# The rests of a split matrix product as float16 instead of float32r, with a re-drawn instruction list

## The chip, the cores and the metric

The kernel runs on one core of a Trainium2 chip. The metric is the device time of one execution in microseconds (us). TensorE is PE in the profile, its loads of the stationary operand are PEld, VectorE is DVE, ScalarE is ACT, GpSimd is POOL, and SP issues the DMAs.

## What is computed

The inputs are x (2 x 1024 x 2048), a context of 2 x 2048 x 2048, a 0/1 matrix `kernel` (2048 x 2048, one entry in ten is 1) and a few scalars. The reference in short:

```python
def fake_quant(x, s, z):
    return (clip(round(x / s + z), 0, 255) - z) * s

x = x + tanh(g_xattn) * (fake_quant(layernorm(x), ...) @ fake_quant(ctx, ...))
y = layernorm(x)                                   # the new x
y = concat([y[..., :1638], -4.0 * y[..., 1638:]])  # 0.8 of the 2048 columns stay
x = x + tanh(g_ffn) * scale * (y @ kernel)
```

So there are two products of 2048 rows by 2048 by 2048. The operands of the first are small integers and go through TensorE as float16 without loss. The left factor of the second is a real float32 matrix, here called A.

## The kernel before

**Tiling.** The 2048 rows are 16 tiles of 128 rows; two tiles make a pair p (0 to 7), two pairs make a product q (0 to 3). All large buffers in SBUF are pages of 4 KB per partition, 44 in all (`page`, `PAGES`). PSUM has three accumulators of 128 x 1024 (`acc`) and two of 128 x 512 (`tr`).

**First product.** Batch 0 is computed directly (`mm1`, line 544) and so is half of batch 1; the other half goes by Strassen's scheme (`mm1s`, line 646), in seven products of halves M1 to M7. All are float16 matmuls of 128 x 128 by 128 x 512. Column sums of the context come from matmuls with ones (lines 556 and 574).

**Second product**, the one that the change touches. For each q the kernel works in Strassen's scheme again:
- `reload2`/`scale2` (line 685) normalise a tile; `factor` (lines 447 to 453) has made the factor r, by a reciprocal and one correction step e.
- `turn2` (line 692) transposes it on TensorE, `take2` (lines 704, 706) moves it from PSUM to a page A, and `combine` (lines 722 to 728) makes the sums of halves.
- `part_hi` (line 738, ACT) rounds A to float32r, and `part_lo` (line 742, DVE or POOL) takes the rest, A - hi, into a page of its own, also as float32r. Each left factor (m, p) has one hi and one lo page.
- `load_w` fetches the right factor as bytes, four k-blocks per page, and `widen` (line 782, ACT) turns each block of 128 x 1024 into float32r (`wf`). The entries are small integers.
- `mm2` (line 809) is the step of TensorE: for one pair and one k-block it issues four matmuls, hi with the left and the right 512 columns, then lo with the same. There are 4 x 7 x 2 x 8 = 448 such steps.
- `add2` (line 825, DVE) adds the accumulator times f2 to a page `back`, and `store2` writes it out.

**The order of the work.** Nothing is scheduled by a compiler. The kernel first describes all operations with their costs, reads, writes and buffers (`op`). `Plan.run` then simulates the engines in units of about a 16-bit matmul's time: each engine takes the ready operation that is due earliest. An operation becomes ready when those it depends on have ended, plus a lag that depends on the releasing engine (`"PE": 6.0`). `Plan.order` repeats this with changed due times (80 tries), keeps the best end, and the instructions are issued in that order, so each engine's queue is fixed when the program is built. A page is opened by one operation and is free when all its users have ended.

Of the kernel before, what the change touches and what calls it, by code (L numbers as in the profile page):

```python
# [22 lines left out]
HB = 1024  # L23
EPS = 1e-5
UNIT = 2.0**-24
CENTER = 128.0
PAGES = 44

# [6 lines left out]
class Plan:  # L35
# [77 lines left out]
    def order(self, lag, start, runs, seed=1):  # L113


        self.dues()
        chance = random.Random(seed)
        free, count = dict(self.free), dict(self.count)
        dues = [o.due for o in self.ops]
        best = None  # L120
        for i in range(runs):
            self.free, self.count = dict(free), dict(count)
            try:
                end = self.run(lag, start)
            except RuntimeError:
                end = None
            if end is not None and (best is None or end <= best[0]):
                best = end, self.began, [o.engine for _, _, o in self.began]
                dues = [o.due for o in self.ops]
                held = self.held_up()  # L130
            for o, due in zip(self.ops, dues):
                o.due = due
            for ops in held:
                if chance.random() < 0.5:
                    step = chance.choice((3.0, 6.0, 12.0, 24.0))
                    for o in ops:
                        o.due -= step
            if i % 3:
                place = chance.uniform(0.0, self.place)
                for o in self.ops:  # L140
                    if o.place is None and abs(o.due - place) < 120.0 and chance.random() < 0.1:
                        o.due += chance.uniform(-25.0, 25.0)
        _, self.began, engines = best
        for (_, _, o), e in zip(self.began, engines):
            o.engine = e
        return [o for _, _, o in self.began]
# [133 lines left out]
def gated_xattn_ffn_kernel(  # L280
# [26 lines left out]

    nc = tc.nc  # L310
    B, S, D = x.shape
    K = kv.shape[1]
# [65 lines left out]
    nc.vector.tensor_scalar(kc12, c1, -CENTER, None, ALU.add)  # L378
    nc.vector.tensor_scalar(kc12, kc12, f1c2, float(K), ALU.mult, ALU.mult)
    f2 = const.tile([P, 1], F32, name="f2")  # L380
    nc.vector.tensor_scalar(f2, gate[:, 1:2], sc[:, 6:7], None, ALU.mult)

    ident = const.tile([P, P], F32, name="ident")
    make_identity(nc, ident)
# [56 lines left out]
    def factor(v, t: int):  # L441


        va, sd = root.pop((v, t))
        mean = mv[v, t][:, 0:1]
        r0 = small.tile([P, 1], F32, tag="r0", name=f"r0_{v}{t}")
        nc.vector.reciprocal(r0, sd)

        e = small.tile([P, 1], F32, tag="e", name=f"e_{v}{t}")
        nc.vector.tensor_scalar(e, r0, r0, va, ALU.mult, ALU.mult)  # L450
        nc.vector.tensor_scalar(e, e, -0.5, 1.5, ALU.mult, ALU.add)
        r = small.tile([P, 1], F32, tag="r", name=f"r_{v}{t}", bufs=T)
        nc.vector.tensor_scalar(r, r0, e, None, ALU.mult)
        fac[v, t] = (r, mean)
        if v == "a":
            w = small.tile([P, 1], F32, tag="w", name=f"w_{v}{t}")
            nc.vector.tensor_scalar(w, va, r, zs1, ALU.mult, ALU.mult)
            nc.vector.tensor_scalar(w, w, mean, None, ALU.subtract)
            nc.vector.tensor_scalar(r, r, rs1, None, ALU.mult)
            wr = small.tile([P, 1], F32, tag="wr", name=f"wr_{v}{t}")  # L460
            nc.vector.tensor_scalar(wr, w, r, None, ALU.mult)
            fac[v, t] = (r, w, wr)
# [275 lines left out]
        nc.scalar.copy(hi[m, p], A[left(m, p)])  # L738

    def part_lo(m: str, p: int, engine=None):  # L740
        lo[m, p] = page([KH, P], F32R, f"lo_{m}_{p}")
        engines[engine].tensor_sub(lo[m, p], A[left(m, p)], hi[m, p].bitcast(F32))  # L742


    RIGHT = {"M1": ("B11", 0), "M2": ("B21", 0), "M3": ("B22", 0), "M4": ("T4", 2),
# [54 lines left out]
    def mm2(q: int, m: str, p: int, k: int, js=(0, 1)):  # L800
        if m in OPENS and k == 0 and apart(p, m):
            acc2[SUM[m], p] = [ps_tr.tile([P, NB], F32, tag="tr", name=f"acc2_{m}_{p}_{j}") for j in range(2)]
        elif m in OPENS and k == 0:
            acc = ps_acc.tile([P, 2, NB], F32, tag="acc", name=f"acc2_{m}_{p}")
            acc2[SUM[m], p] = [acc[:, j, :] for j in range(2)]
            acc2[SUM[m], p, 0] = flat(acc)
        for part in (hi, lo):
            for j in js:
                nc.tensor.matmul(  # L809
                    acc2[SUM[m], p][j],  # L810
                    part[m, p][:, k, :],
                    wf[q, m, k][:, ts(j, NB)],
                    start=(m in OPENS and k == 0 and part is hi),
                    stop=(k == KH - 1 and part is lo),
                    skip_group_check=True,
                )

# [209 lines left out]
    def ops_parts(m: str, p: int):  # L1027
        a = ("A",) + left(m, p)
        op({"ACT": ACT(HB)}, part_hi, m, p, reads=both(a), writes=[(("hi", m, p), 0)],
           opens=[("page", ("hi", m, p))], lead=60)  # L1030
        op({"DVE": DV2(HB), "POOL": GPS(HB)}, part_lo, m, p, reads=[*both(a), (("hi", m, p), 0)],
           writes=[(("lo", m, p), 0)], opens=[("page", ("lo", m, p))], lead=60, port=True)

    def ops_combine(p: int):
        t, u = 2 * p, 2 * p + 1
# [17 lines left out]
    def ops_product2(q: int, between):  # L1053
        pairs = (2 * q, 2 * q + 1)
        for n, m in enumerate(ORDER):
            for j in range(2):
                name = RIGHT[m][0]
                op({"SP": DMA}, load_w, q, m, j, reads=[(("wt", name, j), 0)] if name[0] == "T" else [],
                   writes=[(("wr", q, m, j), 0)], opens=[("page", ("wr", q, m, j))], lead=45)
            for k in range(KH):  # L1060
                w = ("wf", q, m, k)
                op({"ACT": ACT(HB)}, widen, q, m, k, reads=[(("wr", q, m, k // 4), 0)], writes=[(w, 0)],
                   opens=[("page", w)], lead=14)
            if n == 0:
                for p in pairs:
                    ops_combine(p)
            elif n + 1 < len(ORDER):
                for p in pairs:
                    ops_parts(ORDER[n + 1], p)
            if m in FIRST:  # L1070
                for p in pairs:
                    v = ("back", p) + TAKES[m]
                    op({"SP": DMA}, load_back, p, *TAKES[m], reads=[(("kept", 2 * p + TAKES[m][0], TAKES[m][1]), 0)],
                       writes=both(v), opens=[("page", v)], due=plan.place + 50, lead=50)
            steps = [(0, k) for k in range(LAG)]
            for k in range(LAG, KH):
                steps += [(0, k), (1, k - LAG)]
            steps += [(1, k) for k in range(KH - LAG, KH)]

            tail = [(1, k, (j,)) for j in range(2) for k in range(KH - LAG, KH)]  # L1080
            if apart(pairs[1], ORDER[-1]) and n == len(ORDER) - 1:
                steps[-LAG:] = tail
            for i, k, *js in steps:
                p = pairs[i]
                js = js[0] if js else (0, 1)
                acc = ("acc2", SUM[m], p)
                two = apart(p, m)
                keys = [(acc + (j,), 0) if two else (acc, j) for j in js]
                opens = [("tr", acc + (j,)) for j in js] if two else [("acc", acc)]
                op({"PE": 2.1 * len(js)}, mm2, q, m, p, k, js, main=True, writes=keys,  # L1090
                   reads=[(("hi", m, p), 0), (("lo", m, p), 0), (("wf", q, m, k), 0)],
                   opens=opens if m in OPENS and k == 0 else [])
                if k == KH - 1:
                    for js2 in [(j,) for j in js] if two else [js]:
                        v = ("back", p) + TAKES[m]
                        keys = [(acc + (j,), 0) if two else (acc, j) for j in js2]
                        op({"DVE": DV2(len(js2) * NB)}, add2, m, p, js2, reads=keys, writes=[(v, j) for j in js2],
                           due=plan.place)
                        if m in LAST:
                            op({"SP": DMA}, store2, p, *TAKES[m], js2, reads=[(v, j) for j in js2], due=plan.place + 60)  # L1100
            for f, args in between.get(n, ()):
                f(*args)
# [68 lines left out]
    for some in (pairs[:2], pairs[2:]):  # L1171
        for c in range(2, NC):
            for tiles in some:
# [2 lines left out]
    ops_product2(2, {4: [(ops_left, (3, (True, True)))]})  # L1176
    ops_product2(3, {})

    order = plan.order({("ACT", "SP"): 8.0, ("POOL", "SP"): 12.0, ("DVE", "SP"): 12.0, "PE": 6.0, "ACT": 1.5, "DVE": 1.5, "POOL": 1.5, "SP": 4.0, "DMA": 10.0,
                        ("PE", "PE"): 0.0}, {"SP": 13.0, "DVE": 22.0, "ACT": 22.0}, 80, 2)  # L1180
    for o in order:
        if len(o.engines) > 1:
            o.f(*o.args, engine=o.engine)
# [46 lines left out]
```

## Time and profile before

| what | us |
|---|---|
| median of 3 runs (698.67 to 698.84) | 698.72 |
| the profiled execution's own time | 698.79 |
| its span, first to last instruction | 697.0 |
| PE busy | 674.0 |
| DVE busy | 490.2 |
| ACT busy | 455.4 |
| POOL busy | 316.8 |
| mean of one lo call on DVE (x24 of A) | 1.421 |
| mean of one lo call on POOL (x24 of A) | 2.586 |
| first matmul starts | 13.23 |

The span is what the profile's records cover; the rest of the execution's time lies around it. Busy time of PE counts a matmul from its start to its modelled end, so matmuls that follow each other overlap: the pace of a stream is the distance of two starts, not the mean of one. The granted clock was full throughout the span until its last slice.

### The profile page before, as it was taken

The page shows a single profiled execution, that of the slowest core. Times are in us where ns is not written, and L with a number is a line of the kernel's source. Part 1 is how long each engine was busy: PE and PEld are TensorE (multiplying, and loading weights), DVE is VectorE, ACT ScalarE, POOL GpSimd, SP SyncE. Part 2 cuts the span into 40 slices and gives each one's busy share as a digit, 9 for nine tenths or more (in the row PEclk, how much of TensorE's full clock was granted, in tenths as well). Part 3 has the DMA queues.
Part 4 walks back from the last instruction along what each step waited for, and adds up shares of the span by engine and source line. Part 5 has one row for each costly group of instructions (what it writes and reads, how often), then busy time and mean ns, then how long its engine had stood idle before and what let it go on. Part 6 is the DMA issues. An engine that isn't in the chain of part 4 may idle for free.

```text
span 697.0 us, 8833 instructions
## 1 busy us (share of the span) xinstructions
PE 674.0 (97%) x3180; PEld 471.7 (68%) x3180; DVE 490.2 (70%) x717; ACT 455.4 (65%) x536; POOL 316.8 (45%) x210
## 2 busy tenths in 40 slices
PE   1999999989999999999999999999999999999997
PEld 0444444468788888878885444447888888888885
DVE  6899958899998886497878888468572425583331
ACT  4599444286888566699926768229699347689540
POOL 8166789863625221855717887975120101040000
PEclk9999999999999999999999999999999999999999
DMA  8999406777995799477379677327074379155032
GB/s 302 393 393 380 162 13 231 259 261 251 361 400 225 233 324 339 140 247 278 120 263 330 222 268 245 121 92 275 27 260 162 105 231 324 67 170 222 22 131 90
DMA packets 63580, 155.78 MB, mean 223 GB/s; under 512 B 4912, under 2 KB 21296, under 8 KB 63536
## 3 DMA queue, kind: packets, MB, share of 16 engines
q1 hardware_dynamic: 63536, 155.21, 62.9%
q8 instruction: 25, 0.41, 0.2%
q14 instruction: 19, 0.16, 0.1%
HBM read 117.44 MB, written 37.75 MB: 223 GB/s over the span
## 4 chain that ended last, share of the span: by engine, by line
PE 87%; DMA 4%; DVE 4%; POOL 2%; ACT 2%; issue 1%; SPq 0%; ACTq 0%; DVEq 0%
PE acc_M L809 57%; PE acc L544 19%; PE acc_M L646 7%; PE tr L692 4%; DMA kv<-in_kv_dram 3%; DMA x<-in_x_dram 1%; POOL x L596 1%; DVE wB L767 1%; ACT wf_M L782 1%; POOL x L592 1%; PE tr L503 1%; DVE qn L472 0%; PE cs L574 0%; DVE x L685 0%; DVE bn_b L426 0%
## 5 line engine op out<-in xcount | busy, mean ns | idle before, releaser
L809 PE MATMUL acc_M<-wf_M,hi_M 128*128 128x512 f32 x896 | 282.0, 395 | 1.6 <-ACT wf_M L782 1.5
L809 PE MATMUL acc_M<-wf_M,lo_M 128*128 128x512 f32 x896 | 277.6, 390 | 0.6 <-POOL lo_M L742 0.6
L782 ACT ACTIVATE wf_M<-wr_M 128x1024 fp32r<-128x1024 uint8 x224 | 221.6, 1050 | 26.8 <-DMA wr_M<-in_wmask_dram 24.2
L809 PEld LDWEIGHTS acc_M<-wf_M,lo_M 128*128 128x128 f32 x896 | 168.0, 188 | 36.8 <-POOL lo_M L742 1.3
L809 PEld LDWEIGHTS acc_M<-wf_M,hi_M 128*128 128x128 f32 x896 | 164.1, 188 | 34.4 <-ACT wf_M L782 3.2
L544 PE MATMUL acc<-q,q1T 128*128 128x512 f16 x768 | 171.6, 381 | 1.2 <-DVE q1T L514 0.8
L825 DVE SCALAR_TENSOR_TENSOR back<-acc_M,f,back 128x1024 f32<-128x1024 f32 (+1 forms) x58 | 72.1, 1245 | 124.7 <-PE acc_M L809 117.1
L742 POOL TENSOR_TENSOR lo_M<-A,hi_M 128x1024 fp32r<-128x1024 f32 x24 | 62.1, 2586 | 179.5 <-ACT hi_M L738 160.1
L544 PEld LDWEIGHTS <-q1T 128*128 128x128 f16 x768 | 75.2, 98 | 90.2 <-issue 1.9
L592 POOL TENSOR_TENSOR x<-x,row 128x512 f32<-128x512 f32 x64 | 88.6, 1408 | 43.8 <-ACT sd_a L438 15.5
L596 POOL TENSOR_TENSOR x<-x,e 128x512 f32<-128x512 f32 x64 | 92.0, 1458 | 30.6 <-ACT e L586 16.1
L738 ACT CAST hi_M<-A 128x1024 fp32r<-128x1024 f32 x48 | 50.1, 1044 | 13.1 <-POOL A L726 4.7
L530 ACT ACTIVATE q<-kv,sc,rs 128x1024 uint8<-128x1024 f32 x45 | 53.5, 1236 | 7.8 <-DMA kv<-in_kv_dram 5.1
L586 ACT ACTIVATE e<-acc,tokb,f1u 128x512 f32<-128x512 f32 x34 | 25.1, 774 | 49.6 <-PE acc L544 47.8
L426 DVE BATCH_NORM_STATS2 bn_b<-x 128x6 f32<-128x512 f32 x64 | 43.1, 684 | 15.9 <-POOL x L596 15.6
L495 ACT COPY A<-tr 128x512 f32<-128x512 f32 x35 | 20.3, 584 | 46.5 <-PE tr L692 45.8
L742 DVE TENSOR_TENSOR lo_M<-A,hi_M 128x1024 fp32r<-128x1024 f32 x24 | 33.7, 1421 | 7.2 <-ACT hi_M L738 7.2
L568 DVE TENSOR_TENSOR pair<-pair,q 128x1024 f16<-128x1024 f16 x36 | 36.6, 1022 | 2.5 <-ACT q L530 0.8
L728 POOL TENSOR_TENSOR A<-A,A 128x1024 f32<-128x1024 f32 x8 | 21.1, 2648 | 23.7 <-DVE A L726 16.4
L522 POOL MEMSET q<- 128x1024 f32 x32 | 29.2, 952 | 5.1 <-DVE q L532 2.2
L512 ACT ACTIVATE q1T<-tr 128x1024 f16<-128x1024 uint8 x22 | 21.3, 1019 | 7.5 <-PE tr L503 6.8
L767 DVE SCALAR_TENSOR_TENSOR wB<-wB,wB 128x2048 uint16<-128x2048 uint16 x8 | 24.2, 3031 | 0.0
(103 smaller groups left out, 594.1 us busy)
## 6 DMA issues: line engine op xcount, KB each, us to landing
kv<-in_kv_dram SPq DMA_DIRECT2D x64, 512.0 KB, 9.2
x<-in_x_dram SPq DMA_DIRECT2D x32, 512.0 KB, 7.7
x<-x SPq DMA_DIRECT2D x32, 512.0 KB, 3.0
back<-x SPq DMA_DIRECT2D x32, 512.0 KB, 6.1
wr_M<-wt_T SPq DMA_DIRECT2D x32, 512.0 KB, 5.6
out_dram<-back SPq DMA_DIRECT2D x30, 512.0 KB, 3.6
wr_M<-in_wmask_dram SPq DMA_DIRECT2D x24, 512.0 KB, 5.4
n<-in_x_dram SPq DMA_DIRECT2D x16, 512.0 KB, 7.2
```

The source lines that it names most:

```text
L426: nc.vector.bn_stats(bn[v, t][:, c, :], xt[src[v, t, c // 2]][:, ts(c % 2, NB)])
L530: nc.scalar.activation(low, v, AF.Identity, bias=z2, scale=rs2)
L544: nc.tensor.matmul(acc1[b, c, tiles[0]][:, i, :], q1T[tiles[i]][:, k, :], rhs1(b, c, k), start=(k == 0), stop=(k == KT - 1),)
L568: nc.vector.tensor_add(colsum[b, c], colsum[b, c], v[:, i : i + 2, :])
L592: nc.gpsimd.tensor_add(xc, xc, colrow[b, c])
L596: nc.gpsimd.tensor_add(xc, xc, ev.pop((t, c)))
L646: nc.tensor.matmul(acc1[key][:, i, :], left_half(p, LEFT1[m])[:, 4 * s + k, :], right1(m, h, s)[:, k, :], start=(m in OPENS and s == 0 and ...
L738: nc.scalar.copy(hi[m, p], A[left(m, p)])
L742: engines[engine].tensor_sub(lo[m, p], A[left(m, p)], hi[m, p].bitcast(F32))
L782: nc.scalar.activation(wf[q, m, k], wr[q, m, k // 4][:, k % 4, :], AF.Copy, bias=-float(RIGHT[m][1]))
L809: nc.tensor.matmul(acc2[SUM[m], p][j], part[m, p][:, k, :], wf[q, m, k][:, ts(j, NB)], start=(m in OPENS and k == 0 and part is hi), stop= ...
L825: nc.vector.scalar_tensor_tensor(v, acc, f2, v, ALU.mult, ALU.add)
```

## The change

Four things change.
1. **Type of lo.** `part_lo` writes float16. The lo blocks of two pairs of a product share one page; the even pair opens it.
2. **Right factor of the lo matmuls.** They read the upper 16 bits of each float32r value of wf as bfloat16: 512 elements of 2 bytes, 4 bytes apart. The hi matmuls stay as they are.
3. **Scale.** To keep the rests inside float16's range, the factor r of the second layer norm is multiplied by 2^19 (in the immediates of e), and f2 is divided by it.
4. **The list.** The lag behind PE goes from 6 to 2 units, the cost of a step from 2.1 to 2.05 per half, the tries from 80 to 240, and each try changes less: a held-up group with a chance of 0.25 instead of 0.5, and due times within 60 instead of 120 units of a place.

```diff
+BIG = 2.0**19
...
-                if chance.random() < 0.5:
+                if chance.random() < 0.25:
...
-                    if o.place is None and abs(o.due - place) < 120.0 and chance.random() < 0.1:
+                    if o.place is None and abs(o.due - place) < 60.0 and chance.random() < 0.1:
...
-    nc.vector.tensor_scalar(f2, gate[:, 1:2], sc[:, 6:7], None, ALU.mult)
+    nc.vector.tensor_scalar(f2, gate[:, 1:2], sc[:, 6:7], 1.0 / BIG, ALU.mult, ALU.mult)
...
-        nc.vector.tensor_scalar(e, e, -0.5, 1.5, ALU.mult, ALU.add)
+        big = BIG if v == "b" else 1.0
+        nc.vector.tensor_scalar(e, e, -0.5 * big, 1.5 * big, ALU.mult, ALU.add)
...
     def part_lo(m: str, p: int, engine=None):
-        lo[m, p] = page([KH, P], F32R, f"lo_{m}_{p}")
-        engines[engine].tensor_sub(lo[m, p], A[left(m, p)], hi[m, p].bitcast(F32))
+        q, i = p // 2, p % 2
+        if i == 0:
+            lo[m, q] = page([2, KH, P], F16, f"lo_{m}_{q}")
+        engines[engine].tensor_sub(lo[m, q][:, i, :, :], A[left(m, p)], hi[m, p].bitcast(F32))
...
-        for part in (hi, lo):
+        w = wf[q, m, k]
+        upper = w.bitcast(BF).rearrange("p (n b) -> p n b", b=2)[:, :, 1]
+        for part, rhs in ((hi[m, p], w), (lo[m, q][:, p % 2], upper)):
             for j in js:
                 nc.tensor.matmul(
                     acc2[SUM[m], p][j],
-                    part[m, p][:, k, :],
-                    wf[q, m, k][:, ts(j, NB)],
-                    start=(m in OPENS and k == 0 and part is hi),
-                    stop=(k == KH - 1 and part is lo),
+                    part[:, k, :],
+                    rhs[:, ts(j, NB)],
+                    start=(m in OPENS and k == 0 and rhs is w),
+                    stop=(k == KH - 1 and rhs is upper),
                     skip_group_check=True,
                 )
...
-           writes=[(("lo", m, p), 0)], opens=[("page", ("lo", m, p))], lead=60, port=True)
+           writes=[(("lo", m, p // 2), p % 2)], opens=[("page", ("lo", m, p // 2))] if p % 2 == 0 else [],
+           lead=60, port=True)
...
-                op({"PE": 2.1 * len(js)}, mm2, q, m, p, k, js, main=True, writes=keys,
-                   reads=[(("hi", m, p), 0), (("lo", m, p), 0), (("wf", q, m, k), 0)],
+                op({"PE": 2.05 * len(js)}, mm2, q, m, p, k, js, main=True, writes=keys,
+                   reads=[(("hi", m, p), 0), (("lo", m, q), p % 2), (("wf", q, m, k), 0)],
...
-    order = plan.order({..., "PE": 6.0, ...}, {"SP": 13.0, "DVE": 22.0, "ACT": 22.0}, 80, 2)
+    order = plan.order({..., "PE": 2.0, ...}, {"SP": 13.0, "DVE": 22.0, "ACT": 22.0}, 240, 2)
```

More of the change, by code (lines that the diff above doesn't have):

```diff
@@ L119, in order @@
         dues = [o.due for o in self.ops]
-        best = None
+        best, held = None, []
         for i in range(runs):
@@ L1177, in gated_xattn_ffn_kernel @@
     ops_product2(3, {})
-    order = plan.order({("ACT", "SP"): 8.0, ("POOL", "SP"): 12.0, ("DVE", "SP"): 12.0, "PE": 6.0, "ACT": 1.5, "DVE": 1.5, "POOL": 1.5, "SP": 4.0, "DMA": 10.0,
-                        ("PE", "PE"): 0.0}, {"SP": 13.0, "DVE": 22.0, "ACT": 22.0}, 80, 2)
+    order = plan.order({("ACT", "SP"): 8.0, ("POOL", "SP"): 12.0, ("DVE", "SP"): 12.0, "PE": 2.0, "ACT": 1.5, "DVE": 1.5, "POOL": 1.5, "SP": 4.0, "DMA": 10.0,
+                        ("PE", "PE"): 0.0}, {"SP": 13.0, "DVE": 22.0, "ACT": 22.0}, 240, 2)
     for o in order:
```

## The prediction, made before the result was known

> **What bounds the kernel now.** I read the page first: busy shares, then the costliest groups.
>
> ```profile
> PE 674.0 (97%) x3180; PEld 471.7 (68%) x3180; DVE 490.2 (70%) x717; ACT 455.4 (65%) x536; POOL 316.8 (45%) x210
> ...
> L809 PE MATMUL acc_M<-wf_M,hi_M 128*128 128x512 f32 x896 | 282.0, 395 | 1.6 <-ACT wf_M L782 1.5
> L809 PE MATMUL acc_M<-wf_M,lo_M 128*128 128x512 f32 x896 | 277.6, 390 | 0.6 <-POOL lo_M L742 0.6
> ...
> L809 PEld LDWEIGHTS acc_M<-wf_M,lo_M 128*128 128x128 f32 x896 | 168.0, 188 | 36.8 <-POOL lo_M L742 1.3
> ...
> L544 PE MATMUL acc<-q,q1T 128*128 128x512 f16 x768 | 171.6, 381 | 1.2 <-DVE q1T L514 0.8
> ...
> L544 PEld LDWEIGHTS <-q1T 128*128 128x128 f16 x768 | 75.2, 98 | 90.2 <-issue 1.9
> ```
>
> TensorE is the bound, and it hardly waits. A mean of 390 ns is latency, not pace: matmuls overlap. The pace I take from the chain that ended last, as length over count.
>
> ```profile
> 97.41 15.54 PE acc L544 x72
> 112.95 0.87 PE tr L503 x8
> ...
> 506.40 70.77 PE acc_M L809 x312
> ```
>
> So a 16-bit matmul of 512 columns takes 15.54/72 = 215.8 ns, one of float32r 70.77/312 = 226.8 ns, a transpose 0.87/8 = 109 ns. The bill at these paces: 1792 x 226.8 = 406.4 us (L809), 1036 x 215.8 = 223.6 us (L544, L646, L556, L574), 320 x 109 = 35 us, together 665. From the first matmul (13.2 us in) to the last one's end (692.6) are 679.4 us. That leaves 14 us of stalls: about 7 before 50 us, where the DMA row stands near full, 2.5 between 145 and 153 us, the rest scattered.
>
> **The change part by part.**
>
> *The lo matmuls (L809), the main term.* 896 of them become 16-bit: stationary float16, moving the upper halves of wf. If the pace belongs to the matmul alone, that is 896 x (226.8 - 215.8) = 9.8 us less. But the order in mm2 is hi, hi, lo, lo, then the next step's hi: TensorE changes between float32r and 16 bits twice per step, 448 times there and back. The trace has exactly this once, where two f16 matmuls (L574) lie inside the float32r stream. First the matmuls, then the weight loads:
>
> ```profile
> 351.52 0.61 PE L809 MATMUL acc_M<-wf_M,lo_M 128*128 128x512 f32 x2
> 351.98 0.61 PE L574 MATMUL cs<-pair,ones_h 128*128 128x512 f16 x2
> 352.24 0.81 PE L809 MATMUL acc_M<-wf_M,hi_M 128*128 128x512 f32 x2
> 352.89 0.62 PE L809 MATMUL acc_M<-wf_M,lo_M 128*128 128x512 f32 x2
> ```
>
> ```profile
> 351.30 0.41 PEld L809 LDWEIGHTS acc_M<-wf_M,lo_M 128*128 128x128 f32 x2
> 351.98 0.12 PEld L574 LDWEIGHTS <-ones_h 128*128 128x128 f16 x2 [0.26 <-issue]
> 352.21 0.41 PEld L809 LDWEIGHTS acc_M<-wf_M,hi_M 128*128 128x128 f32 x2
> ```
>
> Six matmuls lie between the starts 351.52 and 352.89: 1.37 us. Six of float32r take 1.36; with two at the 16-bit pace it should be 1.338. The reason is in the loads. In the float32r stream a load begins with the matmul before it and is hidden. The first f16 load does not: it waits 0.26 us with nothing to wait for ("issue") and begins only when the float32r matmul has streamed. The same at the only other such edge:
>
> ```profile
> 366.94 0.55 PEld L646 LDWEIGHTS <-q1T 128*128 128x128 f16 x4 [0.26 <-issue]
> 366.95 1.04 PE L646 MATMUL acc_M<-q,q1T 128*128 128x512 f16 x4
> ```
>
> Four matmuls in 1.04 us, the last 0.379 long, leave 0.66 for three starts, 220 ns each and not 215.8: about 13 ns for the way in. To sharpen the first case I laid all PE starts from 333.6 to 366.5 us against a line at 226.55 ns per matmul. They lie 6 ns above it before the f16 pair and 13 ns after it, so the pair took 7 ns (give or take 4) more than two of float32r would. Against its own pace (22 ns saved) a trip there and back thus costs 29 ns, some 14 each way.
>
> Here the Trainium skill is weighed. "TensorE: Matmul & The Clock Gate", in "What happens when you issue a matmul", says that TensorE pulls a weight load ahead of the running matmul and that weights and moving data have separate read ports, so a change of type should be hidden and cost nothing. By the rule: 9.8 us gained. By the two rows: 448 x 29 = 13.0 us paid against 9.8, so +3.2 us. I take the rows, as they are this change's own sequence. Small terms: the last four steps split by halves (four more trips, +0.1), and about 40 places where transposes lie between lo and the next hi. From transposes to float32r the trace shows no loss (transposes at 211.49, lo again at 212.38: 0.89 = 4 x 0.109 + 2 x 0.227), so half a trip is spared there: 40 x 14 = -0.6. **Net +2.7 us**; ends -3.6 (the way back free, only 13 to 14 ns per trip: -9.8 + 6.2) and +5.
>
> *The strided right side.* upper takes 2 bytes out of every 4; no row of the trace has a matmul reading so. The nearest row is the float32r matmul over the same tile and the same bytes: at its pace of 226.8 the lo pair would lose up to 22 ns more, 448 x 22 = +9.8 us. Nothing is to be gained. "SBUF — State Buffer", "SBUF cachelines", asks for at least two hits per 16-byte line for full rate; here four elements share a line, so by the page it is free. I take 0 and keep +9.8 as the end; no run here shows which.
>
> *lo on VectorE and GpSimd (L742).* The same 32 + 32 calls over the same 1024 f32 inputs, half the output bytes. The rows are 1.2 us on DVE and 2.4 on POOL; I take no change. PE waited 0.6 us for a lo, its loads 1.3, so not more than 2 us is to be gained. If a call took half as long again, it would be covered by its lead: POOL idles 180 us of the span ahead of just these calls. The odd pair's lo must follow the even one's, as they share a page: at most one 2.4 us call later, under the same cover.
>
> *Pages.* One page less per left factor in flight, of 44. Only stalls could be won, priced below.
>
> *f2 and e.* The same instructions with other immediates: 0.
>
> *The list (order).* Less wait behind TensorE (6 to 2 units), three times the tries, each with fewer changes, and a PE cost of 2.05. It moves instructions of every queue: loads on SP past each other, evictions on ACT and DVE ahead of widen or hi. What is queued behind an eviction listed early waits on ACT or DVE for TensorE: a semaphore hand-over is short (L578 begins at 352.62, 0.03 us after the second sum's modelled end), so 2 units, about 0.43 us, is still cautious. Gain at most the 7 us of stalls behind 50 us, plus what of the first 50 is not DMA; loss as easily, say the same 7 again. The profile before favours neither, so 0, with ends about -4 and +5.
>
> Sum: the profiled execution has 697.0 of span and 1.8 around it, 698.79; plus 2.7 is 701.5. It stands 0.07 above the median of 698.72, so **701.4 us**. Its own range, with 1.8 us for the pair and 2.5 for the list, is 698.3 to 704.5.
>
> **Rivals.**
> (1) *The change of type is free in the steady stream* (other side). Place: the lo loads of L809. Price: none; the 7 ns of the sums were their own semaphores. Then 698.7 - 9.8 = 689 us. For it: the f16 and float32r paces, and the rule above. Against it: two of two edges with the load held for 0.26 us. It decides as soon as a trip costs under 22 ns.
> (2) *Only the way in costs* (13 to 14 ns): -3.6, about 695 us. For it: the way in is seen twice, the way back once, and transposes to float32r lose nothing. Against it: the 7 ns.
> (3) *The stride costs as well*, or the new list stalls TensorE: 706 to 712 us. The first has no row against it but the page's rule; the second would show as idle PE.
> (4) *The list alone decides*: the pace comes out even and the search takes 3 us off the stalls near 145 to 153 us and at the start: 696 us, inside the range.
>
> **How the numbers follow.** Forecast 0.55, rival 1 0.20, rival 2 with rival 4 0.13, rival 3 0.12. The line between same and not is 0.2%, 1.4 us, about what a measurement of this kernel can tell. Around +2.7 with 3 us of doubt, the forecast's own case splits into faster 0.03, same 0.14, slower 0.38; rival 1 gives faster 0.20; rival 2 and 4 faster 0.10, same 0.02, slower 0.01; rival 3 slower 0.12. Sums: 0.33, 0.16, 0.51. The range reaches from rival 1's 689 to 706; half of rival 1's scatter, half of rival 3, and little else lie outside.
>
> **What would show it.** In the profile after: lo loads near 98 ns instead of 188, and idle before them put down to "issue". In an undisturbed stretch, four matmuls of one step take 0.914 us if I am right, 0.885 if rival 1 is, 0.90 if rival 2, up to 0.93 if the stride costs (now 0.907). PE's stalls should stay near 14 us; if the pace is as said and the time is not, it was the list. I am wrong if loads of f16 are seen beginning with the float32r matmul before them.

## The result and the profile after

The changed kernel takes **707.5 us** (median of 4 runs, 707.29 to 707.86) against 698.7 for the kernel before: a ratio of 1.0126, 95% interval 1.0109 to 1.0144. It is 8.8 us slower. The forecast had the sign right (701.4), but the time lies above the range that ended at 706.

The page of the profiled execution has a span of 706.0 us. These are its rows that answer to those of before (columns: busy us, mean ns of one, idle time before and its cause):

```profile
PE 682.2 (97%) x3180; PEld 355.2 (50%) x3180; DVE 483.6 (68%) x726; ACT 449.3 (64%) x527; POOL 329.5 (47%) x213
...
L820 PE MATMUL acc_M<-wf_M,lo_M 128*128 128x512 bf16 x896 | 281.0, 393 | 2.4 <-DVE lo_M L750 1.3
...
L820 PEld LDWEIGHTS <-lo_M 128*128 128x128 f16 x896 | 52.1, 98 | 125.6 <-issue 121.1
```

TensorE is idle for 23.8 us of this span and was for 23.0 of 697.0 before, so it stalls hardly more. The lo loads take 98 ns instead of 188, as they should, but 121 us of idle time stand before them with no releaser ("issue"). Before, the lo loads had 36.8 us of idle time in front of them and none of it was put down to "issue". The chain that ended last (start, length, count) gives the pace:

```profile
511.44 65.81 PE acc_M L820 x284
...
622.45 78.84 PE acc_M L820 x340
```

65.81/284 = 231.7 ns per matmul, hi and lo together, so a step of four takes 0.927 us (0.927 in the second stretch too). Before it was 0.907. The 20 ns times 448 steps are 9.1 us: the pace of TensorE carries the whole loss. The weight loads of one step and the matmul that the first lo load serves, from the timelines of PEld and PE:

```profile
641.29 0.12 PEld L820 LDWEIGHTS <-lo_M 128*128 128x128 f16 x2 [0.27 <-issue]
641.54 0.41 PEld L820 LDWEIGHTS acc_M<-wf_M,hi_M 128*128 128x128 f32 x2
642.23 0.12 PEld L820 LDWEIGHTS <-lo_M 128*128 128x128 f16 x2 [0.27 <-issue]
...
641.30 0.62 PE L820 MATMUL acc_M<-wf_M,lo_M 128*128 128x512 bf16 x2
```

Each first lo load is held for about 0.27 us and begins only 0.01 us before its own matmul. That is the picture of the two edges in the trace before, now in nearly every step: 446 such waits are counted for 448 steps. But those edges promised 0.914 us per step, not 0.927.

### The profile page after: what moved, and what is told of

Same layout as the page of the kernel before. It is cut to its first block, busy times and chain, and to the rows that moved or that the text cites. A ratio compares the mean times of both kernels' runs of the same rounds, so it can differ in the third digit from the quotient of the medians.

```text
span 706.0 us, 8817 instructions
## 1 busy us (share of the span) xinstructions
PE 682.2 (97%) x3180; PEld 355.2 (50%) x3180; DVE 483.6 (68%) x726; ACT 449.3 (64%) x527; POOL 329.5 (47%) x213
## 4 chain that ended last, share of the span: by engine, by line
PE 85%; DMA 5%; DVE 4%; POOL 3%; ACT 2%; issue 1%; SPq 0%; ACTq 0%; POOLq 0%; DVEq 0%
PE acc_M L820 57%; PE acc L549 16%; PE acc_M L651 7%; PE tr L697 4%; DMA kv<-in_kv_dram 3%; POOL x L601 2%; DMA x<-in_x_dram 2%; DVE wB L775 1%; POOL x L597 1%; ACT wf_M L790 1%; DVE e L593 1%; DVE bn_b L430 1%; PE tr L508 1%; DVE x L690 1%; DVE q1T L519 0%
## 5 line engine op out<-in xcount | busy, mean ns | idle before, releaser
L820 PE MATMUL acc_M<-wf_M,hi_M 128*128 128x512 f32 x896 | 363.3, 487 | 0.4 <-ACT wf_M L790 0.4
L820 PE MATMUL acc_M<-wf_M,lo_M 128*128 128x512 bf16 x896 | 281.0, 393 | 2.4 <-DVE lo_M L750 1.3
L750 POOL TENSOR_TENSOR lo_M<-A,hi_M 128x1024 f16<-128x1024 f32 x27 | 69.9, 2593 | 189.4 <-ACT hi_M L743 169.8
L820 PEld LDWEIGHTS <-lo_M 128*128 128x128 f16 x896 | 52.1, 98 | 125.6 <-issue 121.1
L597 POOL TENSOR_TENSOR x<-x,row 128x512 f32<-128x512 f32 x64 | 90.6, 1436 | 47.9 <-DMA x<-in_x_dram 33.0
L601 POOL TENSOR_TENSOR x<-x,e 128x512 f32<-128x512 f32 x64 | 94.2, 1490 | 31.3 <-DVE e L593 20.5
L535 ACT ACTIVATE q<-kv,sc,rs 128x1024 uint8<-128x1024 f32 x39 | 46.9, 1238 | 13.9 <-DMA kv<-in_kv_dram 8.0
L750 DVE TENSOR_TENSOR lo_M<-A,hi_M 128x1024 f16<-128x1024 f32 x21 | 28.2, 1357 | 2.5 <-ACT hi_M L743 2.5
L537 DVE TENSOR_SCALAR q<-kv,rs,sc 128x1024 uint8<-128x1024 f32 x25 | 23.6, 958 | 2.5 <-DMA kv<-in_kv_dram 2.2
L561 PE MATMUL cs<-q,ones_h 128*128 128x512 f16 x32 | 10.3, 424 | 13.9 <-ACT q L535 13.6
```

The source lines that it names most:

```text
L535: nc.scalar.activation(low, v, AF.Identity, bias=z2, scale=rs2)
L597: nc.gpsimd.tensor_add(xc, xc, colrow[b, c])
L601: nc.gpsimd.tensor_add(xc, xc, ev.pop((t, c)))
L750: engines[engine].tensor_sub(lo[m, q][:, i, :, :], A[left(m, p)], hi[m, p].bitcast(F32))
L820: nc.tensor.matmul(acc2[SUM[m], p][j], part[:, k, :], rhs[:, ts(j, NB)], start=(m in OPENS and k == 0 and rhs is w), stop=(k == KH - 1 and ...
```

## The experiments

Two theories stood for the missing 13 ns per step: (A) the strided right side costs something in each lo matmul; (B) a change of type costs 42 ns there and back in a steady stream, not 29. A rival to both was the new list. In what follows "a trip" is one change from float32r to 16 bits and back. The runs e3 to e8 leave the costs that the planner reads alone, and ACT, DVE, POOL and SP issue the same sequences in all their traces: they have the changed kernel's list, so no new draw of the list lies between them.

**e1_list_only.** Of the change only the list's parameters, on the kernel before:

```diff
-                if chance.random() < 0.5:
+                if chance.random() < 0.25:
-                    ... abs(o.due - place) < 120.0 ...
+                    ... abs(o.due - place) < 60.0 ...
-    order = plan.order({..., "PE": 6.0, ...}, ..., 80, 2)
+    order = plan.order({..., "PE": 2.0, ...}, ..., 240, 2)
```

> The kernel before with the new list alone: lag behind PE of 2, 240 tries with fewer changes each; lo stays float32r in a page per pair, a step stays at 2.1 per half. Theory (the pace of TensorE carries nearly all of the +8.8 us): 698 to 700 us, four matmuls of a step at 0.907 us. Rival (the list costs several us): 703 us or more, with PE stalls above the 14 us of before.

Measured: 708.8 us (707.3 to 710.7), ratio 1.0145 (1.0126 to 1.0163). The theory missed: this list alone costs 10 us on the old types, at an unchanged pace. The last stretches of the two chains, before and e1:

```profile
615.45 77.13 PE acc_M L809 x340
...
624.74 77.13 PE acc_M L809 x340
```

Where the time goes is shown below under e9.

**e2_types_only.** The reverse: the changed kernel with those four parameters put back.

> The changed kernel with the old list parameters (lag 6, 80 tries, the larger changes), so float16 rests, strided right side and shared pages alone. Theory: 707 to 709 us, a step of four matmuls at 0.927 us as in the changed kernel. Rival (the list costs several us): 703 us or less at the same pace.

Measured: 714.2 us, ratio 1.0231 (1.0214 to 1.0248); the step is 0.927 to 0.933 us. The theory missed in this too: 7 us more than the changed kernel. So neither set of parameters is good or bad in itself: the new one costs the old types 10 us and spares the new types 7. Each program gets another draw. The two parts can't be told apart by their sum, only by the pace.

**e3_contiguous.** The stride taken away:

```diff
-        upper = w.bitcast(BF).rearrange("p (n b) -> p n b", b=2)[:, :, 1]
+        upper = w.bitcast(BF)[:, 0:HB]
```

> The changed kernel, whose lo matmuls read 512 adjacent 2-byte elements of the same tile instead of every second one. This changes the computation: the lo products use wrong weights (parts of the first half of each row). List and all else are the same. Theory A (the stride costs the difference between the +7 ns per step of the one f16 pair before and the +20 ns now): 0.914 us per step, 448 x 13 ns less, about 701.5 us. Theory B (the stride is free and the change of type costs 42 ns there and back in a steady stream): 0.927 us per step, 707.5 us.

Measured: 698.7 us, ratio 0.9999 (0.9991 to 1.0008): 8.8 us less than the changed kernel with the same list. Theory B falls. Theory A holds, with 8.8 us instead of the 6 that it asked for. From its chain:

```profile
506.19 63.90 PE acc_M L820 x284
...
614.41 77.68 PE acc_M L820 x340
```

The step is 0.900 us in the first stretch and 0.914 in the second, with the same instructions. The 8.8 us over 896 lo matmuls are 9.8 ns each.

**e4_turned.** Half the trips: every second step is issued lo, lo, hi, hi.

```diff
+        both_parts = [(hi[m, p], w), (lo[m, q][:, p % 2], upper)]
+        if len(steps_done) % 2:
+            both_parts.reverse()
...
```

> The changed kernel with every second step in the order lo, lo, hi, hi, so that TensorE changes type half as often, 224 times there and back. Theory B (price per change of type, 42 ns there and back against 22 ns saved per step): two steps take 2 x 0.885 + 0.042 = 1.812 us instead of 1.854, 448 x 21 ns less, about 698 us. Theory A (the stride slows each lo matmul and a change of type costs 29 ns there and back): 448 x 14.5 ns less, about 701 us. Rival (the pace does not hang on the order): 707.5 us.

Measured: 704.1 us, 3.4 us less than the changed kernel. 3.4/224 = 15 ns for each trip spared, half of what theory A expected and a third of theory B's figure. The time understates it a little: the visible gaps of TensorE are 7.4 us here and 5.7 in the changed kernel.

**e7_doubled.** Twice the trips: hi, lo, hi, lo (the loops over j and over the parts exchanged).

> The changed kernel with a step in the order hi, lo, hi, lo: twice as many changes of type, 896 there and back, all else the same. Theory (13 to 15 ns for each way there and back, the rest of the loss being the stride): 448 x 14 = 6.3 us more than 707.5, about 714 us. Rival (42 ns for each): 448 x 42 = 19 us more, about 726 us.

Measured: 714.0 us, 6.5 us more than the changed kernel, 6.5/448 = 15 ns for each trip added. It agrees with e4.

**e8_turned_contiguous.** e3 and e4 together.

> Adjacent 2-byte elements for lo as in e3_contiguous (wrong weights in the lo products) and every second step turned as in e4_turned: half the changes of type and no stride. Theory (14 to 15 ns per way there and back): 0.885 + 0.007 = 0.893 us per step, about 6 us under the 698.7 of e3_contiguous, 692 us. Rival (without the stride a change of type is free, and the loss of e3 against the pure paces lies elsewhere): 698 us.

Measured: 696.5 us, ratio 0.9969 (0.9959 to 0.9979), 2.2 us under e3: only 10 ns per trip spared, where 6 us in all were expected. The sign holds and the size doesn't. Two steps in a late stretch:

```profile
640.71 1.28 PE L826 MATMUL acc_M<-wf_M,hi_M 128*128 128x512 f32 x4
...
642.52 1.28 PE L826 MATMUL acc_M<-wf_M,hi_M 128*128 128x512 f32 x4
```

Eight matmuls take 1.81 us, so a step takes 0.905 us, not 0.893. What a trip costs is not one number.

**e6_all16_strided.** The stride without any trip: hi is float16 too, with the rest in lo, and all four matmuls read the upper halves of wf.

> The kernel e5_all16 with wf left as float32r and all lo and hi matmuls reading its upper halves, 2 bytes in 4: the stride without any change of type. Theory (the stride costs about 14 ns per matmul by itself): a step of 4 x 0.230 = 0.921 us, about 704 us. Rival (the stride costs only beside changes of type): 0.863 us and 679 us.

**e5_all16.** The same without the stride; `mm2` reads wf itself in all four matmuls:

```diff
-BIG = 2.0**19
+BIG = 2.0**8
...
-        hi[m, p] = page([KH, P], F32R, f"hi_{m}_{p}")
+        hi[m, p] = page([KH, P], F16, f"hi_{m}_{p}")
...
-        wf[q, m, k] = page([HB], F32R, f"wf_{q}_{m}_{k}")
+        wf[q, m, k] = page([HB], F16, f"wf_{q}_{m}_{k}")
...
```

> The changed kernel with every matmul of the second product in 16 bits: hi is float16 too, lo is the float16 rest of it, the scale is 2^8 instead of 2^19, and wf is 1024 adjacent float16 numbers, so no change of type and no stride is left. The same function is computed. Theory (a step costs 4 x 215.8 ns when nothing changes type and nothing is strided): 0.863 us per step against 0.907 before, 448 x 43 ns = 19.4 us less than before, 678 to 681 us. Rival (something else takes the bound, such as ACT, whose widen of 1.05 us serves two steps of 0.863 us): above 685 us, with PE waiting for wf.

Measured: e6 takes 696.0 us (ratio 0.9958, 0.9944 to 0.9972), e5 **680.8 us** (ratio 0.974, 0.9726 to 0.9755), faster than both kernels. The difference is 15.2 us over 1792 matmuls, 8.5 ns each. The timeline of PE in e6, an undisturbed stretch, and the chain of e5:

```profile
640.48 0.61 PE L822 MATMUL acc_M<-wf_M,hi_M 128*128 128x512 bf16 x2
640.93 0.61 PE L822 MATMUL acc_M<-wf_M,lo_M 128*128 128x512 bf16 x2
...
643.64 0.39 PE L822 MATMUL acc_M<-wf_M,lo_M 128*128 128x512 bf16 x1
```

```profile
600.83 73.40 PE acc_M L821 x340
```

In e6, 14 matmuls lie between 640.48 and 643.64: 225.7 ns each. In e5 it is 73.40/340 = 215.9. The stride alone costs 10 ns per matmul, less than the 14 that e6 was expected to show, and it needs no trip. This pair and that of e3 have different weak points: e3 also reads other numbers (wrong weights), and e6 also reads bfloat16 where e5 reads float16 and has ACT write wf at twice the bytes. Both give the same price. The strided pace of 225.7 is within about 1 ns of float32r's 226.8. Both read their numbers at 4-byte steps.

The mean step of each trace puts these runs side by side. It is taken over every stretch of two steps, start to start, without a transpose or a stall in it:

| run | trips per step | right side of lo | mean step, us |
|---|---|---|---|
| before | 0 | float32r | 0.908 |
| changed kernel | 1 | strided | 0.929 |
| e3 | 1 | packed | 0.909 |
| e4 | 1/2 | strided | 0.920 |
| e8 | 1/2 | packed | 0.903 |
| e7 | 2 | strided | 0.944 |
| e6, all in 16 bits | 0 | strided | 0.904 |
| e5, all in 16 bits | 0 | packed | 0.864 |

Half of before and half of e5 make 0.886 us: a step of two float32r and two packed 16-bit matmuls whose trip is free. The stride adds 20 ns to two matmuls, by the changed kernel against e3 and by e6 against e5. A trip in every step adds 23 ns, with the stride or without. Half a trip per step still adds 14 to 17 ns, and two add 38, so the price does not follow the number of trips.

**e9_before_seed3, e10_after_seed3, e11_all16_cost, e12_all16_seed3.** How far lists scatter: the last argument of the search 3 instead of 2 in the kernel before, the changed kernel and e5; and in e11 the cost of a step 2.0 instead of 2.05.

> The kernel before with nothing changed but the seed of its list (3 instead of 2): how far do two lists of the same search lie apart? Theory (the list is a draw with several us of scatter, and the +10 us of e1_list_only is mostly such a draw): 699 to 709 us, at an unchanged step of 0.907 us. Rival (the search reproduces its quality, and the new parameters themselves cost the 10 us): within 2 us of 698.8.

> The changed kernel with seed 3 instead of 2. Theory (a draw): the step stays at 0.927 to 0.934 us and the time moves by 2 us or more either way, most likely up, to 708 to 716. Rival (240 tries settle the list): within 1.5 us of 707.5.

> The kernel e5_all16 with the list told the true cost of a step, 2.0 per half instead of 2.05. A new list with a better model. Theory (a draw): between 676 and 690 us, the step at 0.863 us. If the model's error of 2.5% had cost stalls, 677 to 679 us.

> The kernel e5_all16 with seed 3. Theory (a draw): the step at 0.863 us and a time that differs from 680.8 us by 2 us or more. Rival: within 1.5 us of 680.8.

Measured: e9 700.9 us (ratio 1.0029, 1.0018 to 1.0040), e10 715.2 (1.0229, 1.0203 to 1.0256), e11 684.1, e12 685.5. Seeds alone move these programs by +2, +8 and +5 us, and a truer cost moved e5 by +3. Every list tried is another draw, and the 10 us of e1 lie beyond these four.

The scatter has two parts. The first is stalls: from the first matmul to the last, e1's trace is 9.3 us longer than the one before, and visible gaps make up 6.9 of them (12.2 against 5.3). The gaps are 2.0 of 2.0 us for e9, and against the changed kernel 3.6 of 5.8 for e2 and 3.9 of 9.2 for e10. The second part is seen in e1. The stretch from 150 us on, by windows (width, PE busy (count), PEld, DVE, ACT, POOL, PEclk, DMA share, GB/s), and then its PE timeline:

```profile
150.00:155.00 5.00, 4.08 (x20) 3.12 (x18) 5.00 (x3) 0.50 (x1) 4.19 (x2) 1.00 0.23 85
155.00:160.00 5.00, 1.42 (x6) 1.11 (x7) 5.00 (x7) 2.85 (x3) 0.00 (x0) 0.92 0.98 329
160.00:165.00 5.00, 5.00 (x19) 3.97 (x18) 4.61 (x15) 5.00 (x10) 1.75 (x1) 0.74 0.93 341
```

```profile
157.21 0.63 PE L692 MATMUL tr<-ident,x 128*128 128x128 f32 x4 [3.13 <-DVE A L706]
159.21 1.22 PE L809 MATMUL acc_M<-wf_M,hi_M 128*128 128x512 f32 x2 [1.37 <-ACT wf_M L782]
160.23 1.05 PE L809 MATMUL acc_M<-wf_M,lo_M 128*128 128x512 f32 x2
161.08 1.05 PE L809 MATMUL acc_M<-wf_M,hi_M 128*128 128x512 f32 x2
161.94 0.92 PE L809 MATMUL acc_M<-wf_M,lo_M 128*128 128x512 f32 x2
```

TensorE stands 3.13 us for an A that VectorE delivers late, and 1.37 us more for wf, and with these stalls the granted clock falls (0.92 and 0.74 in the two windows): two matmuls take 0.85 us from start to start (160.23 to 161.08), 425 ns each, until 162.7. The eight matmuls from 159.21 to the next start at 162.70 take 3.49 us instead of 8 x 0.227 = 1.81: 1.7 us on top of the stall. In e10 the clock was 0.50 in the whole of 155 to 160 us, after a wait of 2.6 us:

```profile
154.48 1.22 PE L820 MATMUL acc_M<-wf_M,hi_M 128*128 128x512 f32 x2 [2.61 <-ACT wf_M L790]
```

```profile
155.00:160.00 5.00, 5.00 (x17) 2.81 (x16) 4.24 (x9) 3.79 (x5) 0.70 (x1) 0.50 0.93 368
```

In e2 it was 0.68 and 0.64 in the two windows after 150 us, behind a wait of 3.9 us. In the same windows before, in the changed kernel and in e9 the clock was 1.00; their longest visible gaps there are 1.3 to 1.7 us.

## Why the prediction was right and wrong

**Right: what bounds the kernel.** The loss sits in TensorE's pace, and its visible gaps after the first matmul sum to 5.7 us after and 5.3 before. The "14 us of stalls" were read too simply, though: they are what the bill leaves over, not gaps. Some 3 us of them are the first matmuls, which start about 425 ns apart until 21 us in both kernels, although the clock row shows full speed there.

**Right: the held load and the sign of the first term.** That 16-bit lo would not gain its 9.8 us was read from two edges, and the loads after show the 0.27 us in nearly every step. Rival 1 (a free trip, 689 us) is excluded: without the stride, in e3, a step still takes 0.909 us and not 0.886, and e7 pays 6.5 us for more trips.

**Mis-sized: the price of a trip.** The prediction took 29 ns, so 13.0 us in all and +3.2 net. Measured, it is 23 ns on average (e3, 0.909 - 0.886 us), so 10.3 us in all, which about cancels the saving of 9.8. One f16 pair in one trace was too little to give a price: e3's own stretches show 0.900 and 0.914 us, which are 15 and 29 ns by the prediction's paces, the figures of rival 2 and of the forecast side by side. Nor is the price per trip: one more or one fewer moved the time by 10 ns (e8) or 15 (e4, e7). A part of it lies on the float32r matmuls after a change. In e8's trace near 640 us the second and the third of four in a row still take 230 to 231 ns to the next start, and not 226.8.

**Wrong: the strided right side.** This is the step that failed: "Nothing is to be gained. ... I take 0 and keep +9.8 as the end". The nearest row, float32r over the same bytes, gave 9.8 us; the Trainium skill ("SBUF — State Buffer", "SBUF cachelines") gave 0, as it asks for at least two hits per 16-byte line and four elements share one here. I took the page. Measured: 8.8 us (changed kernel against e3), or 8.5 to 10 ns per matmul (e6 against e5). The measurement decides: the reading is not free. With the row taken, the sum would have been 698.7 + 2.7 + 9.8 = 711 us; with the row and the trip as e3 shows it, 698.7 + 0 + 9.8 = 708.5. Rival 3 gave this at 706 to 712 and got a chance of only 0.12, shared with the list, and the range stopped where that rival began. The prediction's own sign for it, a step of up to 0.93 us, came out at 0.927.

**Lucky: the list.** It was put at 0 with ends of -4 and +5. For this draw that is about right: the gaps grew by 0.4 us, and e3, with the new list and a mean step of 0.909 us, takes the time of before at 0.908. But e1, e2 and e10 show +10, +7 and +8 for neighbours of it: the upper end was half of what it should have been, and the fall of the clock after a long stall was not in the working at all.

**DVE and POOL.** The lo calls on POOL took 2.593 us on average after against 2.586 before, those of A on DVE 1.357 against 1.421: no longer calls, as put. TensorE's matmuls waited 2.4 us for a lo instead of 0.6, though all its gaps together grew by only 0.4 us. That the freed pages help is not shown either way.

**What stays open.** It is not shown why a trip costs 15 ns in one stretch of e3 and 29 in the next, with the same instructions. Nor is it shown whether float32r's slower pace is its 4-byte reading and not its type: e6 fits that within about 1 ns, but no run has float32r without 4-byte steps.

## What to carry to other kernels

In this kernel a narrower type on TensorE paid in full only with a uniform stream and a packed right side. Half the matmuls in 16 bits on a strided view lost 1.3%. The same on packed data came out even (e3), all in 16 bits on a strided view gained 0.4% (e6), and all in 16 bits on packed data gained 2.6% (e5; 1.9% with the slowest of its three lists). Where a page's rule and the nearest row of the trace differ on an operation that was never run, put the sum at the row, or let the range reach it. A re-drawn list is a change by itself with several us of scatter; judge the rest of such a change by the pace in stretches without stalls, at a fixed list.

## What the runs showed of the hardware that was not expected

- A 16-bit right side read at 2 bytes in 4 streams at 225.7 ns per 512 columns, packed at 215.9 (e6, e5).
- The pace of a stream with one trip per step has two levels. In e3 it changes from about 0.914 to 0.900 us per step near 325 us, at four transposes in between (25.58 us for 112 matmuls before them, 27.00 for 120 after), and stays there for the rest of that stretch. The changed kernel changes too at its transposes there, but upwards, from 0.927 (25.97 for 112) to 0.933 (28.00 for 120).
- Around every TensorE stall of 2.6 to 3.9 us after 145 us (e1, e2, e10, e11, e12) the granted clock fell to half; by the windows it stayed there for about 3.4 or 6.8 us, and in e1 that added 1.7 us to the stall of 3.1. Single stalls of 2.1 us (near 302 us in e2, 304 in e10) left it at 1.00. Near 45 us it fell after stalls of 2.0 us (e1) and 1.7 us (e10), to 0.66 and 0.68 over 45 to 50 us, while the same stall of 1.7 us in e12 left it at 1.00. So the length of a stall alone does not decide.
